# A state-space scan after a convolution on one core: projections moved between the scan's steps

## The chip, the core and the metric

The kernel runs on one core of a Trainium2 chip. Five engines work side by side, each through its own queue and in its own order: TensorE (PE, matrix products into PSUM), VectorE (DVE), ScalarE (ACT, activation functions by loaded tables), GpSimd (POOL[...]) and SyncE (SP, which issues DMAs here). They wait for each other on semaphores. The metric is the device time of one execution in microseconds (us); lower is better. All data is 32-bit floating point.

## The reference

The input x is 8 images of 128 channels by 128 x 128. Layer 0 (a dilated convolution, 2D Fourier transforms, an attention over channels and a gate) gives an x of the same shape; the change doesn't touch it. Layer 1 is:

```python
y = conv3x3(x, conv_w) + conv_b
seq = y.reshape(B * H * W, 8, 16)              # 8 tokens of 16 numbers, from consecutive values along W
xi, z = split(seq @ in_proj_w.T)               # 32 each
xc = silu(causal_conv_over_tokens(xi, conv1d_w) + conv1d_b)
dt, Bm, Cm = split(xc @ x_proj_w.T, [1, 17])   # 1, 16, 16
dt = softplus(dt @ dt_proj_w.T + dt_proj_b)    # 32
h = 0
for l in range(8):                             # 32 x 16 states
    h = exp(dt[l] * A) * h + dt[l] * Bm[l] * xc[l]
    ys[l] = sum(h * Cm[l], over the 16)
out = ((ys + D * xc) * silu(z)) @ out_proj_w.T
result = x + silu(groupnorm(out reshaped to the image, 4 groups))
```

As a reader of the reference will see, the tokens of a sequence are 16 consecutive values of one image row, and its 8 tokens fill the row of one channel: channel and image row number the sequences. With channels and rows exchanged by a transposition, one block is 4 rows by 128 channels = 512 sequences.

## The kernel before

Layer 0 runs first (about 3.4 ms). Layer 1 then goes through 8 images x 32 blocks = 256 blocks. The scan of a block is cut in 16 steps, `s` = 0 to 15 (`NS`): token t = s // 2, and half of the 32 inner channels (two of four groups, `GP`) by s % 2. In a step, tiles are 128 partitions (8 channels x 16 states) by 1024 (two groups x 512 sequences). A half `hf` is 4 tokens. `step(i, s)` issues, in this order on each engine, parts of up to four blocks at once, and the order written there is the order of the queues: the body runs under a manual schedule for PE, ACT, DVE, POOL and SP, and the tile framework only adds the waits. For block i and step s:

- `spreads` (L517) for the step after this one: four small matmuls of 16 rows each that spread dt and u over the states, two into `da` (times A, L527) and two into `ups` (L528); then ACT's Exp on da (L530). For token 0 (steps 0 and 1) there is no previous state, so no da and no Exp: step 15 and step 0 issue no exponents. `ups` has one PSUM buffer of two banks, `da` two.
- `advance` (L540): for tokens after the first, DVE multiplies da by the state of two steps earlier (L551) and adds the new input (L552). In the steps of `ON_POOL` (5, 9, 13) the product goes to `ah` (L548) and POOL does the addition (L549).
- `inject` (L533): DVE multiplies ups by B (L537), for the step after this one, into a new h; `weigh` (L554): POOL multiplies h by C into hc (L558).
- `collect` (L561), every second step, four steps later: PE sums hc over the states into `yps` (L568); the first of a half is preceded by the product with D, `m_d` (L566). After the last of a half, `gated` (L572) multiplies by silu(z) on DVE.
- Around these, work of the neighbouring blocks: `project` (L479) for block i + 1 (x, dt, bc and z, each in two halves, one half per step from 0 to 7 by the table `FRONT`), `project_out` (L577) of block i - 1 in step 8, the image convolution `conv` (L460, table `CONV`) and the transposition `turn` (L471) of block i + 2 in steps 9 to 15. All of them take the one buffer of `misc` (L448, `pm`, one bank).
- `lay_out` (L501): SP copies dt, u, B and C of one half to the layout of the scan, in 16 DMAs of 64 or 256 KB. The first half of block i + 1 is laid out in step 8 of block i, the second in step 0 of its own block.
- `keep`, `norm_of` and the `last_...` functions (L588 to L637): statistics, a round trip of the output through DRAM and the final normalization, one block of the image before in each block.

dt, u and bc have one buffer for each half, xc, zs, ym, du, bb and cc have two, h six, hc seven.[...]

Of the kernel before, what the change touches and what calls it, by code (L numbers as in the profile page):

```python
# [9 lines left out]
F32 = mybir.dt.float32  # L10
AF = mybir.ActivationFunctionType
# [5 lines left out]
P = 128  # L17
C = 128
H = 128
W = 128  # L20
# [6 lines left out]
DI = 32  # L27
DS = 16
KC = 4
NG = 4  # L30
LP = 4
NH = 2
# [311 lines left out]
def layer1(ctx, tc, x1, w1, c1, out):  # L344
# [8 lines left out]
    nc = tc.nc  # L353
# [13 lines left out]
    def wf(name):  # L367
        at, n = W1[name]
        return wt[:, at:at + n]
# [13 lines left out]
    m_d = const.tile([P, P], F32, name="m_d")  # L383
# [5 lines left out]
    with tc.tile_pool(name="l1_prep", bufs=2) as prep:  # L389
# [19 lines left out]
        for hf in range(NH):  # L409
            for l in range(L):  # L410
                k = hf * L + l
# [4 lines left out]
    m_xh = m_x.rearrange("p f d l -> p f (d l)")  # L416
    m_zh = m_z.rearrange("p f g l d -> p f (g l d)")
    m_dtf = m_dt.rearrange("p d l -> p (d l)")
# [7 lines left out]
    RB = 4  # L426
    N = RB * C
# [1 line left out]
    NS = L * NG // GP  # L429
    wk1 = ctx.enter_context(tc.tile_pool(name="l1_w1", bufs=1))  # L430
    wk2 = ctx.enter_context(tc.tile_pool(name="l1_w2", bufs=2))
    hp = ctx.enter_context(tc.tile_pool(name="l1_h", bufs=6))
    hcp = ctx.enter_context(tc.tile_pool(name="l1_hc", bufs=7))
    p_u = ctx.enter_context(tc.tile_pool(name="l1_pu", bufs=1, space=PSUM))
    p_a = ctx.enter_context(tc.tile_pool(name="l1_pa", bufs=2, space=PSUM))
    p_m = ctx.enter_context(tc.tile_pool(name="l1_pm", bufs=1, space=PSUM))
# [3 lines left out]
    nb = len(blocks)  # L440
    st8 = [{} for _ in blocks]
    xins, stats, gns, tails = {}, {}, {}, []
    ON_POOL = (5, 9, 13)

    def live(i):
        return 0 <= i < nb

    def misc():  # L448
        return p_m.tile([P, RB, W], F32, name="pm")

    def load(i):
        b, r = blocks[i]
        if r % CH == 0:
            lo, hi = max(0, r - 1), min(H, r + CH + 1)
            xin = wk2.tile([P, CH + 2, W], F32, name="xin")
            nc.sync.dma_start(xin[:, :hi - lo, :], x1[b][:, lo:hi, :])
            xins[b, r // CH] = xin, lo
        st8[i]["xin"] = xins[b, r // CH]
# [17 lines left out]
        d["yT"] = wk1.tile([P, N], F32, name="yT")  # L476
        nc.scalar.copy(d["yT"], ps.rearrange("p a b -> p (a b)"))

    def project(i, what, hf):  # L479
        d = st8[i]  # L480
        ps = misc().rearrange("p a b -> p (a b)")
        if what == "x":
            nc.tensor.matmul(ps, m_xh[:, hf, :], d["yT"], start=True, stop=True)
            d["xc", hf] = wk2.tile([P, N], F32, name=f"xc{hf}")
            nc.scalar.activation(d["xc", hf], ps, AF.Silu, bias=wf("conv1d_b"))  # L485
        elif what == "z":
            nc.tensor.matmul(ps, m_zh[:, hf, :], d["yT"], start=True, stop=True)  # L487
            d["zs", hf] = wk2.tile([P, N], F32, name=f"zs{hf}")
            nc.scalar.activation(d["zs", hf], ps, AF.Silu)
        elif what == "dt":  # L490
            nc.tensor.matmul(ps, m_dtf, d["xc", hf], start=True, stop=True)  # L491
            d["dt", hf] = wk1.tile([P, N], F32, name=f"dt{hf}")
            nc.scalar.activation(d["dt", hf], ps, AF.Softplus, bias=wf("dt_b"))  # L493
            d["u", hf] = wk1.tile([P, N], F32, name=f"u{hf}")
            nc.gpsimd.tensor_mul(d["u", hf], d["dt", hf], d["xc", hf])  # L495
        else:
            nc.tensor.matmul(ps, m_bcf, d["xc", hf], start=True, stop=True)  # L497
            d["bc", hf] = wk1.tile([P, N], F32, name=f"bc{hf}")
            nc.scalar.copy(d["bc", hf], ps)

    def lay_out(i, hf):  # L501

        d = st8[i]
        du = wk2.tile([P, LP, N], F32, name="du")
        bb = wk2.tile([P, LP, N], F32, name="bb")
        cc = wk2.tile([P, LP, N], F32, name="cc")
        for q in range(NG):
            for k, v, g in ((0, d["dt", hf], q), (8, d["u", hf], (q + GP) % NG)):
                nc.sync.dma_start(du[q * DI + k:q * DI + k + 8], v[g * DI:(g + 1) * DI, :])
        for lp in range(LP):  # L510
            for k, v in ((0, bb), (1, cc)):
                at = (k * LP + lp) * DS
                nc.sync.dma_start(  # L513
                    v[:, lp, :], d["bc", hf][at:at + DS, :].unsqueeze(1).broadcast_to([DS, 8, N]))
        d["du", hf], d["bb", hf], d["cc", hf] = du, bb, cc
# [17 lines left out]
    def inject(i, s):  # L533
        d, t = st8[i], s // 2
        bb, lp = d["bb", t // LP], t % LP
        h = hp.tile([P, GP, N], F32, name="h")
        nc.vector.tensor_mul(h, d["ups", s], bb[:, lp:lp + 1, :].broadcast_to([P, GP, N]))  # L537
        d["h", s] = h
# [15 lines left out]
    def weigh(i, s):  # L554
        d, t = st8[i], s // 2
        cc, lp = d["cc", t // LP], t % LP
        hc = hcp.tile([P, GP, N], F32, name="hc")
        nc.gpsimd.tensor_mul(hc, d["h", s], cc[:, lp:lp + 1, :].broadcast_to([P, GP, N]))  # L558
        d["hc", s] = hc

    def collect(i, t):  # L561

        d, hf, lp = st8[i], t // LP, t % LP
        if lp == 0:
            d["yps"] = p_y.tile([P, N], F32, name="yps")
            nc.tensor.matmul(d["yps"], m_d, d["xc", hf], start=True, stop=False, skip_group_check=True)  # L566
        for g in range(NG):
            nc.tensor.matmul(  # L568
                d["yps"][g * DI:(g + 1) * DI], gather[:, lp, :], d["hc", 2 * t + g // GP][:, g % GP],
                start=False, stop=(lp == LP - 1), skip_group_check=True)  # L570

    def gated(i, hf):  # L572
        d = st8[i]
        d["ym", hf] = wk2.tile([P, N], F32, name=f"ym{hf}")
        nc.vector.tensor_mul(d["ym", hf], d["yps"], d["zs", hf])

    def project_out(i):  # L577
        d = st8[i]
        ps = misc()
        for j in range(RB):  # L580
            for hf in range(NH):
                nc.tensor.matmul(  # L582
                    ps[:, j, :], d["ym", hf][:, j * C:(j + 1) * C], m_of[:, hf, :],
                    start=(hf == 0), stop=(hf == NH - 1))
        d["xr"] = wk2.tile([P, RB, W], F32, name="xr")
        nc.scalar.copy(d["xr"], ps)

    def keep(i):  # L588
        d, (b, r) = st8[i], blocks[i]
# [32 lines left out]
    def last_load():  # L622
        b, r, sc, bi = tails.pop(0)
        v = wk2.tile([P, RB, W], F32, name="v")
        res = wk2.tile([P, RB, W], F32, name="res")
        nc.sync.dma_start(v, gns[b][:, r:r + RB, :])
        nc.sync.dma_start(res, x1[b][:, r:r + RB, :])
        fin["now"] = b, r, sc, bi, v, res

    def last_act():  # L630
        b, r, sc, bi, v, res = fin["now"]
        nc.scalar.activation(v, v, AF.Silu, bias=bi, scale=sc)

    def last_sum():
        b, r, sc, bi, v, res = fin.pop("now")
        nc.gpsimd.tensor_add(res, res, v)
        nc.sync.dma_start(out[b, :, r:r + RB, :], res)  # L637

    FRONT = {0: ("x", 0), 1: ("x", 1), 2: ("dt", 0), 3: ("bc", 0), 4: ("dt", 1), 5: ("bc", 1),
             6: ("z", 0), 7: ("z", 1)}  # L640
    CONV = {9: (0, 2), 10: (2, 3), 11: (3, 5), 12: (5, 6), 13: (6, 8), 14: (8, 9)}

    def step(i, s):

        ni, ns = (i, s + 1) if s + 1 < NS else (i + 1, 0)
        if s == 0 and live(i):
            lay_out(i, 1)
        if s == 0 and live(i + 2):
            load(i + 2)
        if live(ni):  # L650
            spreads(ni, ns)
        if s in FRONT and live(i + 1):
            project(i + 1, *FRONT[s])
        if s == 8 and live(i - 1):
            project_out(i - 1)
        if s in CONV and live(i + 2):
            conv(i + 2, *CONV[s])
        if s == 15 and live(i + 2):
            turn(i + 2)
        if live(i):  # L660
            advance(i, s)
        if live(ni):
            inject(ni, ns)
        if live(i):
            weigh(i, s)

        gi, gs = (i, s - 4) if s >= 4 else (i - 1, s - 4 + NS)
        if gs % 2 == 0 and live(gi):
            collect(gi, gs // 2)
        if gs in (7, 15) and live(gi):  # L670
            gated(gi, gs // 8)
        if s == 8 and live(i + 1):
            lay_out(i + 1, 0)
        if s == 1 and tails:
            last_load()
        if s == 7 and fin:
            last_act()
        if s == 8 and fin:
            last_sum()
        if s == 9 and live(i - 1):  # L680
            keep(i - 1)
        if s == 15 and live(i - 1) and blocks[i - 1][1] + RB == H:
            norm_of(blocks[i - 1][0])

    E = mybir.EngineType
    with tc.manual_schedule(engines={E.PE, E.Activation, E.DVE, E.Pool, E.SP}):
        for i in range(-2, nb + 1):
            for s in range(NS):
                step(i, s)
    while tails or fin:  # L690
        if not fin:
            last_load()
        last_act()
        last_sum()


def network(tc, x, w0, w1, c0, c1, out):
# [79 lines left out]
```

## Time and profile before

| | |
|---|---|
| Median of 3 runs | 19010.8 us (18965.37 to 19032.3) |
| Profiled execution, its own time | 18927.41 us |
| Its span, first to last instruction | 18925.6 us |
| PE busy | 17631.7 us (93%) |
| DVE busy | 13871.6 us (73%) |
| POOL busy | 12629.5 us (67%) |
| ACT busy | 10176.7 us (54%) |
| PE's mean granted clock | 0.891 |
| DMA, mean share of 16 engines | 47.3% on the queue of SP |

Busy shares are means over both layers. A busy PE isn't a PE at its peak, since the ends of matmuls are modelled and PE's clock can be throttled. Each float32 matmul stands in the trace as two records. In a line of groups, the two numbers behind the bar are busy time and the mean duration of one in ns, then the idle time of that engine just before and what ended it. In a timeline the columns are start, duration, engine, line and operation, with the idle time before it in brackets.

### The profile page before, as it was taken

To read this page: it belongs to the slowest core of one execution; us is meant where nothing else is said; L and a number is where in the kernel's file an instruction comes from. 1 tells how busy PE (TensorE), PEld (TensorE's weight loads), DVE (VectorE), ACT (ScalarE), POOL (GpSimd) and SP (SyncE) were. 2 spreads that over 40 slices of the span, in tenths; PEclk is the share of its full clock that TensorE was granted. 3 is DMA by queue.
4 is the path that set the end of the run, shared out by engine and by line. 5 is a ranking of instruction groups with operands and counts; after the bars stand their busy time and mean duration, and the time that the engine had idled before them with its cause. 6 is when DMAs were issued, how large, how long until landed. Compare 5 with 4: busy or idle time off the path is not lost.

```text
span 18925.6 us, 214060 instructions
## 1 busy us (share of the span) xinstructions
PE 17631.7 (93%) x74920; PEld 6394.7 (34%) x74920; DVE 13871.6 (73%) x14203; ACT 10176.7 (54%) x10759; POOL 12629.5 (67%) x5892
## 2 busy tenths in 40 slices
PE   8999999999999999999999999999999999999996
PEld 3554553333333333333333333333333333333332
DVE  1441437888887888878888888878888878888885
ACT  1221225565565565565665565666565565565564
POOL 0010115777777777777877777777777777777776
PEclk9999999888888888888888888888888888888887
DMA  2222224554555555555555555555555555555554
GB/s 87 71 76 77 78 75 92 95 98 93 101 109 106 108 109 108 106 106 111 108 109 108 105 107 111 107 107 110 106 111 106 107 107 108 107 108 110 107 109 121
DMA packets 1075829, 1933.33 MB, mean 102 GB/s; under 512 B 123968, under 2 KB 255040, under 8 KB 1058368
## 3 DMA queue, kind: packets, MB, share of 16 engines
q1 hardware_dynamic: 1001472, 1850.17, 47.3%
q10 hardware_dynamic: 73280, 69.47, 1.3%
q8 instruction: 594, 9.73, 0.2%
q14 instruction: 483, 3.96, 0.1%
HBM read 375.64 MB, written 201.33 MB: 30 GB/s over the span
## 4 chain that ended last, share of the span: by engine, by line
PE 54%; DVE 7%; SPq 6%; POOL 5%; DMA 4%; ACT 4%; issue 3%; POOLq 0%; ACTq 0%; DVEq 0%
PE da L527 14%; PE yps L568 8%; PE pm L134 8%; PE ups L528 8%; SPq L513 6%; POOL hc L558 5%; PE pm L582 4%; PE pm L491 3%; PE yps L566 3%; PE pm L497 3%; DVE h L537 3%; DMA cc<-bc 2%; DVE da L551 2%; PE pm L487 2%; DMA bb<-bc 2%
## 5 line engine op out<-in xcount | busy, mean ns | idle before, releaser
L558 POOL TENSOR_TENSOR hc<-h,cc 128x1024 f32<-128x1024 f32 x4096 | 9578.2, 2356 | 1046.9 <-issue 671.2
L537 DVE TENSOR_TENSOR h<-ups,bb 128x1024 f32<-128x1024 f32 x4096 | 4987.1, 1218 | 2538.7 <-PE ups L528 1765.2
L530 ACT ACTIVATE da<-da 128x1024 f32<-128x1024 f32 x3584 | 3612.7, 1008 | 4562.6 <-PE ups L528 4546.2
L528 PE MATMUL ups<-du,m_u 16*128 16x512 f32 x16384 | 5185.2, 699 | 442.8 <-DVE h L537 438.5
L527 PE MATMUL da<-du,m_a 16*128 16x512 f32 x14336 | 5529.0, 683 | 11.4 <-DVE h L552 2.8
L551 DVE TENSOR_TENSOR da<-da,h 128x1024 f32<-128x1024 f32 x2816 | 3447.3, 1224 | 153.5 <-ACT da L530 129.3
L552 DVE TENSOR_TENSOR h<-da,h 128x1024 f32<-128x1024 f32 x2816 | 3448.1, 1224 | 96.7
L527 PEld LDWEIGHTS da<-du,m_a 16*128 16x128 f32 x14336 | 1700.8, 195 | 3351.2 <-issue 1476.8
L568 PE MATMUL yps<-hc,l_ct 128*32 128x512 f32 x16384 | 2633.3, 720 | 3.0 <-POOL hc L558 3.0
L134 PE MATMUL pm<-xin,l_wt 128*128 128x508 f32 (+1 forms) x4608 | 2368.0, 623 | 5.1 <-DMA l_wt<-w 4.4
L495 POOL TENSOR_TENSOR u<-dt,xc 128x512 f32<-128x512 f32 x512 | 651.1, 1272 | 2534.5 <-ACT dt L493 2445.4
L530 ACT ACT_TABLE_LOAD x1531 | 1964.3, 1283 | 27.6
L528 PEld LDWEIGHTS ups<-du,m_u 16*128 16x128 f32 x16384 | 1411.4, 197 | 1240.4 <-DVE h L537 1172.7
L549 POOL TENSOR_TENSOR h<-ah,h 128x1024 f32<-128x1024 f32 x768 | 1815.0, 2363 | 1.7
L134 PEld LDWEIGHTS pm<-xin,l_wt 128*128 128x128 f32 x4608 | 750.7, 189 | 1528.7 <-issue 1475.5
L272 POOL TENSOR_TENSOR xr<-xr,sq 128x512 f32<-128x512 f32 x128 | 160.7, 1267 | 1649.2 <-ACT sq L271 1604.7
L548 DVE TENSOR_TENSOR ah<-da,h 128x1024 f32<-128x1024 f32 x768 | 935.1, 1218 | 186.0 <-ACT da L530 181.9
L134 PE MATMUL cps<-xin,l_wt 128*64 128x500 f32 (+2 forms) x4608 | 1023.6, 583 | 38.7 <-issue 30.4
L491 PE MATMUL pm<-xc,m_dt 128*128 128x512 f32 x1024 | 838.4, 912 | 139.6 <-ACT xc L485 138.7
L222 DVE COPY fT<-tps 128x512 f32<-128x512 f32 x128 | 88.6, 692 | 1179.2 <-PE tps L221 1179.2
L568 PEld LDWEIGHTS yps<-hc,l_ct 128*32 128x32 f32 x16384 | 346.5, 116 | 1679.6 <-issue 1263.6
L497 PE MATMUL pm<-xc,m_bc 128*128 128x512 f32 x1024 | 601.9, 671 | 257.2 <-ACT dt L493 257.2
(146 smaller groups left out, 15341.6 us busy)
## 6 DMA issues: line engine op xcount, KB each, us to landing
bb<-bc SPq DMA_DIRECT2D x2048, 256.0 KB
cc<-bc SPq DMA_DIRECT2D x2048, 256.0 KB
du<-dt SPq DMA_DIRECT2D x2048, 64.0 KB
du<-u SPq DMA_DIRECT2D x2048, 64.0 KB
xin<-x SPq DMA_DIRECT2D x112, 640.0 KB
xin<-x SPq DMA_DIRECT2D x48, 1408.0 KB
gn<-xr SPq DMA_DIRECT2D x256, 256.0 KB
v<-gn SPq DMA_DIRECT2D x256, 256.0 KB
```

Source lines behind the costliest of these rows:

```text
L134: nc.tensor.matmul(out[:, a:b, wa:wb], wt[:, t, :], src[:, r + dy + a - base:r + dy + b - base, wa + dx:wb + dx], start=(n == 0), stop=(n ...
L491: nc.tensor.matmul(ps, m_dtf, d["xc", hf], start=True, stop=True)
L497: nc.tensor.matmul(ps, m_bcf, d["xc", hf], start=True, stop=True)
L527: nc.tensor.matmul(da[:, q], m_a[a:a + 16, :], du[a:a + 16, lp, :], start=True, stop=True)
L528: nc.tensor.matmul(ups[:, q], m_u[u:u + 16, :], du[u:u + 16, lp, :], start=True, stop=True)
L530: nc.scalar.activation(da, da, AF.Exp)
L537: nc.vector.tensor_mul(h, d["ups", s], bb[:, lp:lp + 1, :].broadcast_to([P, GP, N]))
L549: nc.gpsimd.tensor_add(h, ah, h)
L551: nc.vector.tensor_mul(da, da, before)
L552: nc.vector.tensor_add(h, da, h)
L558: nc.gpsimd.tensor_mul(hc, d["h", s], cc[:, lp:lp + 1, :].broadcast_to([P, GP, N]))
L568: nc.tensor.matmul(d["yps"][g * DI:(g + 1) * DI], gather[:, lp, :], d["hc", 2 * t + g // GP][:, g % GP], start=False, stop=(lp == LP - 1), ...
```

## The change

The projections are done for both halves at once, 1024 wide, in PSUM buffers of `da`. x and z of block i + 2 are projected in step 15 (before it: one half a step, of block i + 1, in steps 0, 1, 6 and 7), dt of block i + 1 in step 0 (before: steps 2 and 4), bc in steps 1 and 2 (before: 3 and 5). The product u = dt * xc goes from POOL, by halves, to DVE, in one. `project_out` is cut in two, steps 5 and 6. The product with D is moved from the first matmul of a half in yps to the last, just ahead of `gated`. `ON_POOL` has four steps instead of three. The convolution's and the transposition's steps, and those of the last normalization, are moved. Buffers: h five, hc six; xc and zs three of double width, dt and u two of double width, ym one for each half; bc0 and bc1 stay at one.

```diff
-    hp = ctx.enter_context(tc.tile_pool(name="l1_h", bufs=6))
-    hcp = ctx.enter_context(tc.tile_pool(name="l1_hc", bufs=7))
+    wk3 = ctx.enter_context(tc.tile_pool(name="l1_w3", bufs=3))
+    hp = ctx.enter_context(tc.tile_pool(name="l1_h", bufs=5))
+    hcp = ctx.enter_context(tc.tile_pool(name="l1_hc", bufs=6))
...
-    ON_POOL = (5, 9, 13)
+    ON_POOL = (5, 8, 11, 14)
...
-    def project(i, what, hf):
+    def halves(m, rhs):
+
+        ps = p_a.tile([P, NH, N], F32, name="da")
+        for hf in range(NH):
+            nc.tensor.matmul(ps[:, hf], m[hf], rhs[hf], start=True, stop=True)
+        return ps
+
+    def project_x(i):
+        d = st8[i]
+        ps = halves([m_xh[:, hf, :] for hf in range(NH)], [d["yT"]] * NH)
+        d["xc"] = wk3.tile([P, NH, N], F32, name="xc")
+        nc.scalar.activation(d["xc"], ps, AF.Silu, bias=wf("conv1d_b"))
+
+    def project_z(i):
+        d = st8[i]
+        ps = halves([m_zh[:, hf, :] for hf in range(NH)], [d["yT"]] * NH)
+        d["zs"] = wk3.tile([P, NH, N], F32, name="zs")
+        nc.scalar.activation(d["zs"], ps, AF.Silu)
+
+    def project_dt(i):
+        d = st8[i]
+        ps = halves([m_dtf] * NH, [d["xc"][:, hf, :] for hf in range(NH)])
+        d["dt"] = wk2.tile([P, NH, N], F32, name="dt")
+        nc.scalar.activation(d["dt"], ps, AF.Softplus, bias=wf("dt_b"))
+
+    def inputs(i):
+        d = st8[i]
+        d["u"] = wk2.tile([P, NH, N], F32, name="u")
+        nc.vector.tensor_mul(d["u"], d["dt"], d["xc"])
+
+    def project_bc(i, hf):
...
+        nc.tensor.matmul(ps, m_bcf, d["xc"][:, hf, :], start=True, stop=True)
+        d["bc", hf] = wk1.tile([P, N], F32, name=f"bc{hf}")
+        nc.scalar.copy(d["bc", hf], ps)
...
-            nc.tensor.matmul(d["yps"], m_d, d["xc", hf], start=True, stop=False, skip_group_check=True)
...
-                start=False, stop=(lp == LP - 1), skip_group_check=True)
+                start=(lp == 0), stop=False, skip_group_check=True)
+
+    def skip(i, hf):
+        d = st8[i]
+        nc.tensor.matmul(d["yps"], m_d, d["xc"][:, hf, :], start=False, stop=True, skip_group_check=True)
...
-    FRONT = {0: ("x", 0), 1: ("x", 1), 2: ("dt", 0), 3: ("bc", 0), 4: ("dt", 1), 5: ("bc", 1),
-             6: ("z", 0), 7: ("z", 1)}
-    CONV = {9: (0, 2), 10: (2, 3), 11: (3, 5), 12: (5, 6), 13: (6, 8), 14: (8, 9)}
+    CONV = {7: (0, 2), 8: (2, 3), 9: (3, 5), 10: (5, 6), 11: (6, 7), 12: (7, 8), 13: (8, 9)}
+    OUT = {5: (0, 5), 6: (5, 8)}
...
-        if s in FRONT and live(i + 1):
-            project(i + 1, *FRONT[s])
-        if s == 8 and live(i - 1):
-            project_out(i - 1)
+        if s == 15 and live(i + 2):
+            project_x(i + 2)
+        if s == 0 and "loaded" in fin:
+            last_act()
+        if s == 0 and live(i + 1):
+            project_dt(i + 1)
+        if s in (1, 2) and live(i + 1):
+            project_bc(i + 1, s - 1)
+        if s in OUT and live(i - 1):
+            project_out(i - 1, *OUT[s])
         if s in CONV and live(i + 2):
             conv(i + 2, *CONV[s])
-        if s == 15 and live(i + 2):
+        if s == 14 and live(i + 2):
             turn(i + 2)
         if live(i):
             advance(i, s)
         if live(ni):
             inject(ni, ns)
+        if s == 1 and live(i + 1):
+            inputs(i + 1)
         if live(i):
             weigh(i, s)
+        if s == 15 and live(i + 2):
+            project_z(i + 2)
...
+            if gs in (7, 15):
+                skip(gi, gs // 8)
+                gated(gi, gs // 8)
```

Left out of the diff: the loop runs three blocks ahead instead of two; the last normalization's load goes from step 1 to step 8, its Silu from step 7 to step 0 (between z's Silu and dt's Softplus in ACT's queue), its sum from step 8 to step 3; `keep` goes from step 9 to 7.

## The prediction

> **What bounds the kernel now.** I read the page's clock row and costliest groups, the trace around one block (10011.8 to 10074.7 us), the throttle's records, and the issue times of SP. Layer 1 does 256 blocks; three in turn repeat every 184.3 us, so one takes 61.4 us.
>
> ```profile
> PEclk9999999888888888888888888888888888888887
> L537 DVE TENSOR_TENSOR h<-ups,bb 128x1024 f32<-128x1024 f32 x4096 | 4987.1, 1218 | 2538.7 <-PE ups L528 1765.2
> L530 ACT ACT_TABLE_LOAD x1531 | 1964.3, 1283 | 27.6
> ```
>
> Eight tenths in layer 1: TensorE's clock is part of the bound. Steps 2 to 8 run at ScalarE's pace, two loads around each projection, and PE waits for the result:
>
> ```profile
> 10028.29 1.28 ACT L493 ACT_TABLE_LOAD   x1
> 10029.59 0.69 ACT L493 ACTIVATE dt<-pm,l_wt 128x512 f32<-128x512 f32 x1
> 10030.29 1.28 ACT L530 ACT_TABLE_LOAD   x1
> 10031.58 1.01 ACT L530 ACTIVATE da<-da 128x1024 f32<-128x1024 f32 x1
> ...
> 10030.33 1.12 PE L497 MATMUL pm<-xc,m_bc 128*128 128x512 f32 x2 [1.13 <-ACT dt L493]
> ```
>
> Steps 10 to 15 run at DVE's pace, starts 1.25 + 1.14 + 1.14 = 3.53 us apart, while PE is nearly full:
>
> ```profile
> 10057.45 1.22 DVE L551 TENSOR_TENSOR da<-da,h 128x1024 f32<-128x1024 f32 x1
> 10058.70 1.22 DVE L552 TENSOR_TENSOR h<-da,h 128x1024 f32<-128x1024 f32 x1
> 10059.84 1.21 DVE L537 TENSOR_TENSOR h<-ups,bb 128x1024 f32<-128x1024 f32 x1
> 10060.97 1.22 DVE L551 TENSOR_TENSOR da<-da,h 128x1024 f32<-128x1024 f32 x1
> ```
>
> Busy time by stretch (length; PE, PEld, DVE, ACT, POOL; clock; DMA share, GB/s), cut at the throttle's edges:
>
> ```profile
> 10015.41:10022.24 6.83, 6.83 (x18) 1.75 (x22) 1.22 (x1) 2.16 (x3) 5.88 (x3) 0.50 0.79 122
> 10022.24:10032.47 10.23, 8.50 (x43) 2.56 (x38) 8.85 (x8) 9.41 (x9) 2.12 (x2) 1.00 0.89 196
> 10032.47:10039.30 6.83, 6.83 (x23) 1.55 (x17) 4.77 (x5) 4.89 (x6) 5.32 (x4) 0.50 0.25 94
> ```
>
> The clock is whole or half. Matmuls at half clock lost this block 3.2, 2.4 and 1.7 us; 62.96 - 7.3 = 55.7 us at full clock (a two-window block: 58.4 - 3.4 = 55.0).
>
> I weighted matmul time by the array's rows and columns in use (16 of 128 rows in the spreads, 32 of 128 columns in the collects). Between 6000 and 15900 us, 412 full-clock windows before a drop had at most 0.46; of 1794 without a drop, 95% had over 0.56 and none under 0.44. Half clock ended after windows with at least 0.88 of their own time, 0.44 of the full rate. So each 3.41 us window needs some 1.5 us of full-array work; at half clock it must be nearly all dense work, which four spreads (2.1 us, worth 0.53) spoil.
>
> [...]
>
> **The change, part by part.** Let T = 0 be the end of inject(15); hand-offs 0.05 us.
>
> Loads: twelve per block (around x, dt, z twice each) become three in the instruction list: 9 x 1.28 = 11.5 us less ACT. Two 512-wide calls become one: about 0.3 us less, three times.
>
> DVE: u moves here (1.22, the 1024-wide row), a fourth POOL step removes one add (1.14). Even.
> POOL: minus 2.54, plus 2.36: even.
> PE: the same matmuls. x, z and dt (2.1 us each at full clock) go to steps 15 and 0; output, 2.05 us whole, to 5 and 6; convolution to 7 to 13. m_d moves behind the collects, and gated waits for it. In step 3 PE has room (m_d ends at 18.9, gated is due at 20.3). In step 11 it hasn't: spreads(12) starts when inject(11) ends, 1.05 us, then tap and m_d 2.1; DVE meanwhile needs only 2.49 to gated, so it waits 0.65 us. The other edges cost nothing: the output projection's halves lie in steps with room on PE, the copy to xr waits in ACT's idle time (ACT is busy some 25 us of the block once the loads are gone), and the fewer h and hc buffers suffice, since POOL is at most four steps behind DVE when inject(s+1) needs weigh(s-4), and the collect that frees a slot of hc stands two steps earlier in PE's queue. The prologue's extra round is a few us once.
>
> The boundary in a row, no longer under exponents:
> PE: collect until 0.35, spreads(0) to 1.4, x to 3.5, z to 5.6, spreads(1) to 6.7, dt to 8.8, collect to 9.8, spreads(2) to 10.9, bc0 to 11.9.
> ACT: x to 4.7, z to 6.7, last Silu (0.80) to 7.5, load to 8.8, Softplus 8.9 to 10.0, load to 11.3, exp(2) to 12.3.
> DVE: inject(2) 10.9 to 12.05, u to 13.25, then advance(2).
> From there DVE alone: nine steps of 3.53, four POOL steps of 2.49 (13 before), three of gated and bn_stats at 0.60: 31.8 + 10.0 + 1.8 = 43.6. Sum 56.85 us, with step 11's wait 57.5.
>
> A wait added: bc1 is copied in step 2 instead of 5, and still has one buffer, which lay_out(i,1) of step 0 is reading. Its DMAs now (T = 11.8):
>
> ```profile
> 10010.01 0.74 SPq L509 DMA_DIRECT2D du<-dt  x1
> ...
> 10026.01 1.58 SPq L513 DMA_DIRECT2D cc<-bc  x1
> ```
>
> By the DMA packets (2 KB, 256 of du and 1024 of bb and cc) the last lands at 10031, T + 19.2. After, spreads(15) frees du 0.5 us later, and cc waits for POOL's hc(15) at 6.0: T + 20.1. Behind the copy on ACT stands exp(4), for which DVE waits: 20.1 + 0.59 + 1.01 = 21.7 against 20.9 when advance(4) is due: 0.9. Bounds: 0 (landing under 19) to 5 (packets under load took 70 to 300 ns). Base: 58.4 us at full clock, about 3 over before's: the boundary's chain x, z, Softplus, exp, u holds DVE idle 7 us, where before's projections lay beside DVE's work.
>
> Clock A: steps 3 and 4 have only spreads with m_d or a collect, 2.1 us of 4.1 and 4.5: activity 0.33 to 0.46. The drop comes at 18 to 23 (three alignments of the window grid worked through). It is hidden until 25.3, inject(5); then PE sets the pace at half clock: spreads(6) 2.1, output 2.1, spreads(7) 2.1, output and collect 3.3, spreads(8) 2.1, convolution 4.0. The spreads stand at 25.3, 29.5 and 34.9, so a window dense enough comes only in the 3.3 or the 4.0. With window edges at 31.9 and 35.3 it is the former: spreads(8) then ends at 36.2 and inject(8) at 37.4, due at 34.85, 2.5 late. With edges at 36.4 and 39.8, or 37.5 and 41.0, it is the convolution: inject(9) ends at 42.6 or 43.2, due at 37.9, 4.7 or 5.3 late. Mean 4.2. DVE has no room to win it back. Bounds 0 and 8 (another two steps at half clock).
>
> Clock B: step 13 has spreads and one tap, 2.1 of 3.53: 0.39 to 0.46 by the alignment. I give it one half. The drop then comes about T - 1, and the next window free of spreads lies within x and z, which run on PE's path at half clock to about T + 8: 8.2 us at half cost 4.1, 2.05 on the mean.
>
> Sum: 58.4 + 4.2 + 2.05 = 64.65 us; 3.25 more per block, x 256 = 830 us on the profiled execution's 18,927 us (span 18,925.6). Layer 0 is untouched. That execution lies 83 us under the median of the runs; to that I add the same: 19,010.8 + 830 = about 19,840 us.
>
> **Rivals.** *The clock holds* (faster): steps 3 to 6 keep over 1.5 us of dense work in each window, because DVE's steps there are shorter than I made them. Place: ups L528 of steps 4 to 8; price: A and B go, 58.4 us, 256 x -3.0 = -770, 18,240; with A at 1.5 and no B, 59.9, 18,630. For it: over layer 1 (3524 to 18655 us) ACT was busy 9075 us, 37 of each block's 61.4, and 11.5 of these go. Against: the 10.23 us stretch above, PE idle 1.7 us, was followed by half clock. It decides from A + B under 3.0 us.
> *The DMA wait is long*: bb and cc land at T + 25, five us past advance(4)'s need, and PE idles until then. 4 us more per block: 20,880. For: DMA at 0.8 to 0.9 in just that stretch; against: the queue starts when it does now.
> *Gains and losses cancel*: A at 2.5 and B rare give 58.4 + 2.5 + 0.5 = 61.4, 19,010. For: before pays about 6 us to the clock too.
> That the loads stay is excluded by the instruction list.
>
> **How the numbers follow.** Forecast (62.7 to 66.3 us a block; 19,350 to 20,260): 0.55. Longer, mostly the DMA wait: 0.12. Cancelling (60.9 to 62.7; 18,900 to 19,350): 0.18, of which 0.06 within 0.3% (18,954 to 19,068, about what a measurement of this kernel can tell) and 0.02 below. Clock holds: 0.15. So faster 0.17, same 0.06, slower 0.77. The range leaves out some 0.10 under 18,800 and 0.10 above 20,350; the forecast's own is 19,350 to 20,260.
>
> **What would show it.** Table loads near 800; POOL without u; half clock in about a third of layer 1, with drops in steps 3 and 4; ACT's bc1 copy idle up to T + 20, released by DMA; ups L528 waiting for inject in steps 3 to 5. Wrong if the clock row shows nines in layer 1, if bc1's copy waits beyond T + 22, or if x and z don't follow each other on PE.

## The result, and the profile after

The changed kernel takes 19149.9 us (median; 19125.35 to 19192.02) against 18999.18 us for the kernel before on the same chip: ratio 1.0082, 95% interval 1.0056 to 1.0108. It is slower, as forecast, but by 0.8% where 4.4% were forecast, inside the wide range (18,800 to 20,350) and outside the likeliest case's own (19,350 to 20,260). The profiled execution of the changed kernel (span 19190.2 us) happens to be its longest; per block of the scan its mean is 62.73 us, that of the kernel before 61.76 us (means over all 255 distances between the ends of inject(15), image ends among them).

The page's clock row, one of its costliest groups, and the table loads among the groups by line, as before:

```profile
PEclk9999998888888888888888888888888888888886
L553 DVE TENSOR_TENSOR h<-ups,bb 128x1024 f32<-128x1024 f32 x4096 | 4993.9, 1219 | 2903.9 <-PE ups L544 2546.7
...
L546 ACT ACT_TABLE_LOAD x263 | 337.4, 1283 | 240.0 <-issue 206.9 <-PE ups L544 32.9
L491 ACT ACT_TABLE_LOAD x256 | 328.4, 1283 | 4.5
L503 ACT ACT_TABLE_LOAD x256 | 328.4, 1283 | 4.6
```

Three loads a block instead of twelve; ACT is busy 3144 us less. That bought no time: DVE's idle time before inject rose from 2539 to 2904 us (the part put down to PE from 1765 to 2547), and the clock row is no better (the granted clock of layer 1 fell from 0.878 to 0.844).

One block, from the end of inject(15) at T = 10020.45 us to the next at 10081.85 us. ACT and DVE at the boundary and behind it (start, duration, engine, line, operation, idle time before):

```profile
10029.89 1.11 ACT L503 ACTIVATE dt<-da,l_wt 128x1024 f32<-128x1024 f32 x1
10031.94 1.28 ACT L546 ACT_TABLE_LOAD   x1 [0.93 <-issue]
10033.24 1.01 ACT L546 ACTIVATE da<-da 128x1024 f32<-128x1024 f32 x1
...
10040.41 0.59 ACT L515 COPY bc<-pm 128x512 f32<-128x512 f32 x1 [4.74 <-DMA xin<-x]
10040.89 1.02 ACT L546 ACTIVATE da<-da 128x1024 f32<-128x1024 f32 x1
```

```profile
10028.02 1.23 DVE L553 TENSOR_TENSOR h<-ups,bb 128x1024 f32<-128x1024 f32 x1 [3.48 <-PE ups L544]
10032.01 1.23 DVE L553 TENSOR_TENSOR h<-ups,bb 128x1024 f32<-128x1024 f32 x1 [2.76 <-PE ups L544]
10033.15 1.22 DVE L508 TENSOR_TENSOR u<-dt,xc 128x1024 f32<-128x1024 f32 x1
...
10041.34 0.68 DVE L594 TENSOR_TENSOR ym<-yps,zs 128x512 f32<-128x512 f32 x1
10041.94 1.23 DVE L567 TENSOR_TENSOR da<-da,h 128x1024 f32<-128x1024 f32 x1
...
10047.84 1.22 DVE L553 TENSOR_TENSOR h<-ups,bb 128x1024 f32<-128x1024 f32 x1 [1.14 <-POOL hc L574]
10052.31 1.23 DVE L553 TENSOR_TENSOR h<-ups,bb 128x1024 f32<-128x1024 f32 x1 [0.85 <-PE ups L544]
10057.17 1.23 DVE L553 TENSOR_TENSOR h<-ups,bb 128x1024 f32<-128x1024 f32 x1 [1.24 <-PE ups L544]
```

And PE across the block's end, then its spreads for inject(6):

```profile
10018.43 0.73 PE L544 MATMUL ups<-du,m_u 16*128 16x512 f32 x1
10019.09 1.11 PE L476 MATMUL pm<-l_ct,y 128*128 128x128 f32 x4
10020.14 1.94 PE L583 MATMUL yps<-hc,l_ct 128*32 128x512 f32 x8
10022.00 1.18 PE L544 MATMUL ups<-du,m_u 16*128 16x512 f32 x4
10023.12 1.98 PE L484 MATMUL da<-yT,m_x 128*128 128x512 f32 x4
10024.94 1.88 PE L484 MATMUL da<-yT,m_z 128*128 128x512 f32 x4
...
10046.64 1.06 PE L544 MATMUL ups<-du,m_u 16*128 16x512 f32 x1
```

The order of the prediction's boundary is all there. inject(2) starts at T + 11.6 (forecast 10.9), bc1's copy at T + 20.0, when a DMA ends ACT's idle time (forecast 20.1), advance(4) at T + 21.5 (21.7). Then three injects in a row wait while PE is at half clock. The view puts the first of these waits down to POOL, but POOL's product ended at 10047.0, and the last spread that this inject reads at 10047.7. The busy time by stretch, cut where the granted clock changes (columns as before):

```profile
10018.75:10022.16 3.41, 3.41 (x17) 1.07 (x14) 3.10 (x4) 2.88 (x3) 3.33 (x3) 0.50 0.11 43
10022.16:10042.64 20.48, 19.88 (x78) 6.02 (x82) 13.71 (x13) 10.45 (x11) 13.32 (x6) 1.00 0.75 154
10042.64:10056.29 13.65, 13.61 (x52) 5.88 (x56) 11.20 (x10) 3.61 (x4) 10.94 (x7) 0.50 0.11 41
10056.29:10080.19 23.90, 23.61 (x108) 6.74 (x100) 22.10 (x20) 7.74 (x8) 20.49 (x9) 1.00 0.69 131
```

The prediction's two drops (stretches at half clock) are there, A at T + 22 for four windows of 3.413 us, B at T - 1.7 for one. The stretches add up to 61.44 us, exactly 18 windows of 3.413 us. The windows are read from the traces: from 4000 us on the granted clock of both kernels is 0.5 or 1.0, and every change of it (1232 before, 959 after) lies within 0.01 us of one grid of 3.413 us.

### The profile page after: what moved, and what is told of

Read it like the earlier page. It is cut to its first block, busy times and chain, and to the rows that moved or that the text cites. A ratio compares the mean times of both kernels' runs of the same rounds, so it can differ in the third digit from the quotient of the medians.

```text
span 19190.2 us, 208781 instructions
## 1 busy us (share of the span) xinstructions
PE 18443.3 (96%) x74920; PEld 6645.5 (35%) x74920; DVE 13878.4 (72%) x14203; ACT 7032.3 (37%) x7703; POOL 12632.6 (66%) x5636
## 5 line engine op out<-in xcount | busy, mean ns | idle before, releaser
L543 PE MATMUL da<-du,m_a 16*128 16x512 f32 x14336 | 6343.9, 728 | 210.0 <-DVE h L568 193.2
L544 PE MATMUL ups<-du,m_u 16*128 16x512 f32 x16384 | 5410.2, 737 | 9.7 <-DVE h L553 2.6
L568 DVE TENSOR_TENSOR h<-da,h 128x1024 f32<-128x1024 f32 x2560 | 3134.0, 1224 | 87.8
L567 DVE TENSOR_TENSOR da<-da,h 128x1024 f32<-128x1024 f32 x2560 | 3132.2, 1224 | 65.0 <-ACT da L546 62.8
L583 PE MATMUL yps<-hc,l_ct 128*32 128x512 f32 x16384 | 2824.9, 769 | 1.7 <-POOL hc L574 1.7
L565 POOL TENSOR_TENSOR h<-ah,h 128x1024 f32<-128x1024 f32 x1024 | 2420.7, 2364 | 392.0 <-DVE ah L564 391.8
L564 DVE TENSOR_TENSOR ah<-da,h 128x1024 f32<-128x1024 f32 x1024 | 1240.9, 1212 | 0.0
L602 PEld LDWEIGHTS pm<-m_o,ym 128*128 128x128 f32 x4096 | 909.7, 327 | 767.1 <-issue 766.3
L602 PE MATMUL pm<-m_o,ym 128*128 128x128 f32 x4096 | 1060.1, 440 | 0.6 <-DVE ym L594 0.6
L515 ACT COPY bc<-pm 128x512 f32<-128x512 f32 x512 | 301.6, 589 | 1041.0 <-DMA cc<-bc 594.9
```

What stands on the lines that cost most here:

```text
L543: nc.tensor.matmul(da[:, q], m_a[a:a + 16, :], du[a:a + 16, lp, :], start=True, stop=True)
L544: nc.tensor.matmul(ups[:, q], m_u[u:u + 16, :], du[u:u + 16, lp, :], start=True, stop=True)
L564: nc.vector.tensor_mul(ah, da, before)
L565: nc.gpsimd.tensor_add(h, ah, h)
L567: nc.vector.tensor_mul(da, da, before)
L568: nc.vector.tensor_add(h, da, h)
```

## The experiments

Theory: at full clock the changed block is about 58.4 us against 55 to 56 before (its boundary is a chain on which DVE waits, with a DMA wait and D's wait behind it), and half clock adds to both. Rivals: half clock is only a by-product of waits; or the clock alone makes the difference; or the table loads did set the pace before, and the gain was eaten elsewhere. The means per block and the half-clock time per block are from each run's trace, the ratios to the kernel before from the runs timed beside each.

| run | median us | ratio (95%) | us per block | of it half clock |
|---|---|---|---|---|
| before | 18999.2 | | 61.76 | 15.0 |
| changed | 19149.9 | 1.0082 (1.0056-1.0108) | 62.73 | 19.6 |
| before_fill | 17462.1 | 0.9187 (0.9169-0.9204) | 56.03 | 1.1 |
| before_thin | 18418.6 | 0.9722 (0.9701-0.9743) | 59.73 | 9.3 |
| before_exp | 18229.9 | 0.9590 (0.9576-0.9605) | 59.03 | 12.1 |
| before_fill_exp | 17349.3 | 0.9162 (0.9148-0.9175) | 55.60 | 1.6 |
| fill_a | 18914.2 | 0.9951 (0.9935-0.9966) | 61.63 | 10.8 |
| fill_ab | 18959.7 | 0.9983 (0.9974-0.9991) | 61.78 | 11.2 |
| fill_all | 18109.8 | 0.9567 (0.9552-0.9581) | 58.50 | 0.7 |
| fill_all_bc | 17873.5 | 0.9439 (0.9424-0.9453) | 57.60 | 0.5 |
| fill_all_d | 18618.6 | 0.9828 (0.9791-0.9865) | 60.53 | 5.4 |
| fill_bc_d | 18033.1 | 0.9518 (0.9499-0.9537) | 58.24 | 0.5 |
| fill_bc_d2 | 17817.5 | 0.9400 (0.9383-0.9416) | 57.40 | 0.5 |
| bc_two | 18914.0 | 0.9983 (0.9976-0.9991) | 61.72 | 17.7 |

**Holding the clock with work that nothing uses.** In the changed kernel's `spreads`, a dense matmul into the bank of da that the spread is about to overwrite:

```diff
+        if s in (4, 5, 6):
+            for q in range(1):
+                nc.tensor.matmul(da[:, q], m_bcf, d["xc"][:, 0, :], start=True, stop=True)
         for q in range(GP):
             g = k * GP + q
```

> The changed kernel with one more dense matmul (128 rows, 512 columns, 1.05 us at full clock) on PE ahead of the spreads of tokens' steps 4, 5 and 6, written into the da bank that the spread overwrites; its result is used by nothing. PE has 1.5 to 3 us of idle time there. Clock theory (half clock in steps 4 to 8 costs the block 3 to 4 us, because PE does too little in steps 3 and 4): the drop that began 22 us after inject(15) goes, block 62.7 to about 59.5 us, time about 18,400 (18,200 to 18,600). Rival, the chain of waits alone sets the time and half clock is its by-product: within 0.3% of the changed kernel, 19,100 to 19,200. Rival, PE is full: 3 x 1.05 us more per block, 19,950.

Measured 18914 us, not 18,400. Drop A is gone from 246 of 255 blocks, but B now lasts three windows in those 246, and the block is 61.44 us again: 18 windows. With `(4, 5, 6, 14, 15)`:

> As before it, and such matmuls ahead of the spreads of steps 14 and 15 too, where the second drop (in steps 13 and 14) comes from. Clock theory: no drop is left or nearly none, block near the full-clock sum of 57.5 to 58.4 us, time about 18,000 (17,850 to 18,250), clock in layer 1 above 0.95. Rival, only the first drop costs: as fill_a, 18,400. By-product rival: 19,100 to 19,200.

Measured 18960 us. B is gone and A is back, at T + 25. The 13 blocks without any drop took 57.71 us. So neither first forecast held: taking away one drop let the other grow. I put A's return down to idle time of PE between step 4's collect and the next da bank, an estimate; fill_all puts two more matmuls there, at the end of step 4:

```diff
+        if s == 4 and live(i):
+            ps = misc().rearrange("p a b -> p (a b)")
+            for k in range(2):
+                nc.tensor.matmul(ps, m_bcf, st8[i]["xc"][:, k, :], start=True, stop=True)
```

> The changed kernel with dense matmuls that nothing uses ahead of the spreads of steps 4, 5, 6, 14 and 15 (one each, into da) and two more at the end of step 4 (into pm), so that no 3.4 us window on PE is nearly empty. Theory that the arrangement itself is longer at full clock (57.5 us a block by the prediction's sum without its DMA wait, against 55.5 measured for the kernel before with its own fill): 17,462 + 2.0 x 256 = 17,975 (17,900 to 18,100), no half clock but at image ends. Rival, only the clock makes the change slower: 17,460 or less. With the 0.9 us DMA wait: 18,200.

Measured 18110 us, with no drop in 244 of 255 blocks, which took 58.2 us on the mean. That is the changed kernel's block at full clock, DMA wait and all; the forecast's base was 58.4. Nothing of it is the price of the two matmuls in step 4, which lie behind the DMA wait: inject(6) follows inject(5) at DVE's own pace, 2.5 us. The same with the kernel before, one matmul ahead of five of its spreads:

```diff
+        if s in (1, 3, 4, 5, 9):
+            w = da if t else p_a.tile([P, GP, N], F32, name="da")
+            nc.tensor.matmul(w[:, 0], m_bcf, d["xc", 0], start=True, stop=True)
```

> The kernel before with the same extra dense matmul ahead of the spreads of steps 1, 3, 4, 5 and 9 (5 x 1.05 us of PE a block), where its own low windows lie. Clock theory: drops mostly gone, from 61.7 to 56 to 59 us, 17,550 to 18,300. Rival, PE full in these steps or ACT's loads the bound whatever the clock: the matmuls come on top or change nothing, 19,000 to 20,300.

Measured 17462 us, below the expected range: 8.1% faster than the kernel before by adding work to its busiest engine. From its page, and the stretch of one block:

```profile
PEclk9999999999999999999999999999999999999997
L540 DVE TENSOR_TENSOR h<-ups,bb 128x1024 f32<-128x1024 f32 x4096 | 4983.7, 1217 | 1070.8 <-PE ups L531 957.0
L530 PE MATMUL da<-du,m_a 16*128 16x512 f32 x14336 | 4726.0, 644 | 1.8 <-DVE h L555 1.7
```

```profile
10000.00:10055.50 55.50, 53.74 (x256) 17.96 (x259) 50.20 (x45) 36.85 (x39) 48.00 (x23) 1.00 0.62 125
```

55.50 us a block in 229 of 255 blocks, all at full clock, and DVE's idle time before inject down from 2539 to 1071 us. DVE is now busy 50.2 of 55.5. The kernel before itself has five blocks without a drop in its trace, and they take 55.48 us: so the unused matmuls change the clock and hardly anything else. Half clock is thus no by-product: it costs the kernel before 5.7 us a block (61.76 - 56.03) and the changed one 4.2 (62.73 - 58.50). And the clock isn't all: at full clock the changed block is 2.5 us longer.

Is it the array's activity, or just a busy PE? The same five matmuls with 16 rows instead of 128:

```diff
-            nc.tensor.matmul(w[:, 0], m_bcf, d["xc", 0], start=True, stop=True)
+            o = k * GP * 32
+            nc.tensor.matmul(w[:, 0], m_a[o:o + 16, :], d["xc", 0][o:o + 16, :], start=True, stop=True)
```

> The kernel before with the five extra matmuls of before_fill in the same places and of the same length (512 columns), but of 16 rows instead of 128. Theory that the clock goes by how much of the array works (rows and columns weighted): an eighth of the activity each, the drops stay, 18,700 to 19,600. Rival, the time that PE is busy counts, or the extra instructions change the order of waits: near before_fill's 17,462.

Measured 18419 us, below the expected range: about a third of before_fill's gain for as many instructions of the same length (ratios 0.9722 and 0.9187). 65 blocks had no drop and took 55.48 us; most others kept two drops. So rows count. That an eighth of the rows gives a third of the gain is no contradiction, for the traces show a limit. They were weighted as in the prediction, each matmul record with 0.53 us for 512 columns at full clock (half of the 1061 ns that the median dense record took at half clock), times its shares of the array's rows and columns, as a share of the window. The limit of 0.46, which the prediction had from the kernel before alone, tells whether the next window is at half or full clock in all but 213 of the 55,150 windows of the 13 other kernels (from 4000 us to the last block). Over all 14 kernels the best single limit, 0.465, fails in 248 of 59,481 windows; on rows alone it fails in 2303, on PE's busy share in 6280. By that weighting a thin matmul adds an estimated 0.04 to a window (two records of 0.53 us, / 8 / 3.41), and of the kernel before's 614 windows ahead of a drop 168 lay within 0.04 of the limit; 346 drops are left in before_thin, 27 in before_fill.

**What the table loads cost.** Silu as Identity, Softplus as Exp in layer 1 (z and the last normalization likewise), so these kernels compute other values; they leave out the loads:

```diff
-            nc.scalar.activation(d["xc", hf], ps, AF.Silu, bias=wf("conv1d_b"))
+            nc.scalar.activation(d["xc", hf], ps, AF.Identity, bias=wf("conv1d_b"))
...
-            nc.scalar.activation(d["dt", hf], ps, AF.Softplus, bias=wf("dt_b"))
+            nc.scalar.activation(d["dt", hf], ps, AF.Exp, bias=wf("dt_b"))
```

> The kernel before with layer 1's Silu replaced by Identity and Softplus by Exp, so that ACT loads no table inside a block (computation changed: the activations of x, z, dt and of the last normalization are other functions; same instructions otherwise). Theory that the loads set the pace of steps 2 to 8: twelve loads, 15.4 us of ACT, go; PE no longer waits for the projections, block 61.7 to 56 to 58.5 us, time 17,550 to 18,200. Rival, the loads lay beside work that is needed anyway: block over 60.5, time over 18,700.

> The kernel before with the fill matmuls, and Silu as Identity and Softplus as Exp in layer 1 (other functions, no table load inside a block). What twelve loads cost when the clock holds. If they lie beside DVE's and PE's work, as the 0.5 us waits of DVE for ACT suggest: 1 to 2 of them show, block 54.5 to 55.3, 17,200 to 17,420. If they set the pace of steps 2 to 8: block under 53.5, under 16,950.

Without the loads the kernel before takes 18230 us (between the two forecasts). With the clock held, 17349: the typical block goes from 55.50 to 54.82 us. Twelve loads, 15.4 us of ACT a block, show as 0.7 us: they lie beside DVE's work. Of the 2.7 us that they cost with the clock free (61.76 - 59.03), the larger part, 2.7 - 0.7 = 2.0 us, goes with the clock (half clock fell from 15.0 us a block to 12.1); why it fell isn't shown. So there was little in the loads for the change to win.

**The DMA wait.** Two buffers for each half of bc, in the changed kernel and in fill_all:

```diff
-        d["bc", hf] = wk1.tile([P, N], F32, name=f"bc{hf}")
+        d["bc", hf] = wk2.tile([P, N], F32, name=f"bc{hf}")
```

> As fill_all, with two buffers for each half of bc, so that bc1's copy in step 2 no longer waits for the DMAs that read the block before's. The prediction's term: 0.9 us a block, 230 us less than fill_all. Rival, read from the changed kernel's trace (advance(4) started when gated ended, not later): the wait is hidden, within 50 us of fill_all.

> The changed kernel with two buffers for each half of bc and nothing else. With the clock held this was worth 0.9 us a block (18,110 to 17,874). Reading of the changed kernel's trace: under half clock at the block's start the copy comes late anyway and advance(4) is not held up, so nothing is gained: 19,050 to 19,200. Rival, the prediction's sum, where waits and clock add up: 18,920.

With the clock held: 58.50 - 57.60 = 0.90 us, the forecast's number, though not its sum, as the table below shows. In fill_all's view of the waits ACT's copy stands with these lines (us in total, times, longest); in fill_all_bc its waits for DMA come to 16 us in all:

```profile
ACT bc L515 <- DMA cc<-bc: 1099.0, 175, 7.7
...
ACT bc L515 <- DMA xin<-x: 145.9, 21, 16.3
```

Alone in the changed kernel, two buffers save 1.0 us a block (62.73 to 61.72), where I had expected nothing. Medians over blocks of one kind show where the two savings come from (us after T; the last column is the block's length):

| blocks | inject(2) | bc1's copy | inject(5) | next T |
|---|---|---|---|---|
| fill_all, no drop (244) | 10.1 | 20.1 | 24.1 | 58.2 |
| fill_all_bc, no drop (246) | 10.1 | 14.1 | 22.5 | 57.3 |
| changed, B of one window (167) | 11.5 | 20.1 | 24.1 | 61.6 |
| changed, B of three windows (82) | 14.4 | 19.9 | 26.8 | 64.3 |
| bc_two, B of one window (238) | 11.6 | 15.5 | 23.9 | 61.4 |

With the clock held, the DMA wait holds inject(5) back by 1.6 us, not 0.9; in fill_all_bc the unused matmuls of step 4, now uncovered, take 0.7 us back before inject(6) (DVE waits 0.92 us there, 0.20 in fill_all). Under half clock the wait and B lie in one chain, and the copy stands at T + 20.1 with B or without it: a B of one window makes inject(2) 1.4 us late, and the DMA wait swallows all of it. In bc_two, where nothing swallows it, inject(5) comes 1.4 us later than in fill_all_bc, and a block of that kind is only 0.2 us shorter than the changed kernel's. Most of its 1.0 us is that the long drops went: 85 of 255 blocks of the changed kernel have a B of three windows or more, 13 of bc_two. Why they went isn't shown; the typical block of bc_two, 61.46 us on the mean in 217 blocks, is 18 windows long.

**D last.** In fill_all, then in fill_all_bc, the product with D first in yps as before the change; fill_bc_d and fill_bc_d2 have one more unused matmul in step 3, where it had stood, and the latter one less in step 4:

```diff
         if lp == 0:
             d["yps"] = p_y.tile([P, N], F32, name="yps")
+            nc.tensor.matmul(d["yps"], m_d, d["xc"][:, t // LP, :], start=True, stop=False, skip_group_check=True)
...
-                skip(gi, gs // 8)
                 gated(gi, gs // 8)
```

> As fill_all, with the product with D first in yps again, as before the change. Theory that D last costs DVE 0.65 us in step 11, where gated waits for it: 165 us less than fill_all. Rival, the matmul is missed or paid in step 12 instead: within 50 us of fill_all.

> As fill_all_bc, with the product with D first in yps again, and one more unused dense matmul at the end of step 3, where the product with D had stood, so that the clock holds there. D last costs 0.65 us in step 11 by the prediction: block 57.3 to 56.7, 17,874 - 165 = 17,710. Rival, the wait moves to step 12, where PE now has one matmul more: within 50 us of 17,874.

> As fill_bc_d, with one unused matmul in step 4 instead of two, so that steps 3 and 4 hold as much PE work as in fill_all_bc (the product with D has taken the place of one there). fill_bc_d's trace has DVE's 0.64 us wait for yps in step 11 gone, 0.51 us more in step 14 and 1.05 us more before inject(6), where the extra matmul stood. Theory that the order of D moves the wait and hardly its sum: block 57.1 to 57.4, within 50 us of fill_all_bc's 17,874. Prediction's term alone: 17,710. If D first is dearer in itself: 18,000.

fill_all_d was inconclusive: taking the matmul out of step 3 brought drop A back at T + 19 in 198 blocks (18619 us), and the 56 blocks without a drop took 58.1 us, as in fill_all. fill_bc_d came out slower (18033), for the extra matmul in step 4 stood before inject(6), where DVE waited 1.97 us against 0.92. fill_bc_d2 holds the work of steps 3 and 4 equal: typical block 57.14 against 57.32, 0.2 us (56 us by the timed runs, just over the 50 of the forecast). DVE's waits say where the rest went. The first line is fill_all_bc, the second fill_bc_d2 (times are those of two executions):

```profile
10040.99 0.69 DVE L597 TENSOR_TENSOR ym<-yps,zs 128x512 f32<-128x512 f32 x1 [0.64 <-PE yps L592]
```

```profile
10028.55 1.22 DVE L556 TENSOR_TENSOR h<-ups,bb 128x1024 f32<-128x1024 f32 x1 [0.51 <-PE ups L547]
```

gated's 0.64 us is gone and 0.51 us stand before inject(15), put down to its spreads on PE. From step 12 to there PE's queue holds the product with D and two unused matmuls, of steps 13 and 14. So with this fill the wait moved. Whether D first would keep its 0.64 us where nothing unused stands in PE's way wasn't run without the drops.

## Why the prediction was right or wrong

- *Loads, engines' sums*: right. Three loads a block; DVE 13,878 us against 13,872; POOL even.
- *Boundary*: right in order, and 0.8 us shorter than forecast: at full clock inject(2) starts at T + 10.1, not 10.9. ACT's three 1024-wide calls (x, z, dt), which the row has at 1.1 to 1.2 us, took 1.11, 1.02 and 1.11 in the changed kernel's block.
- *DMA wait, 0.9*: right in cause, and bc1's copy stands at T + 20.1 as forecast. That exp(4) stands behind it on ACT is shown by the block above: the copy starts at 10040.41, exp(4) at 10040.89, and advance(4) follows on DVE at 10041.94. Its price at full clock is 1.6, because the boundary before it is shorter; that the experiment gave 0.90 is luck, since unused matmuls hid the rest.
- *Step 11's wait, 0.65*: right in the trace (0.64). As a price of D last it isn't settled: with the fill, D first pays 0.51 of it in step 14.
- *Base 58.4*: right as a sum, 58.2 in the blocks of fill_all without a drop; the boundary's - 0.8 and the DMA wait's + 0.7 cancel. For before's 55.0 to 55.7, 55.48 and 55.50. That PE would go to half clock in steps 3 and 4 held too, and when, in the blocks with B of one window (T + 21.9; forecast 18 to 23).
- *Clock A 4.2 and B 2.05*: the step that failed. Together they cost 62.73 - 58.50 = 4.2 us where 6.25 stood. A came in nearly every block and cost 3.4: from inject(5) to the next T a block takes 37.5 us, with B of either length, against 34.1 in fill_all. I had given three alignments of the window grid one weight each; the block settles on the grid (140 of 255 blocks have B of one window and A of four, 79 B of three and A of four, and nearly all others are variants of these), and both kinds are cheaper than the mean of the three. B's full price was right, 4.3 us at inject(2) where it lasts three windows (forecast 4.1), but it did so in a third of the blocks. B came in nearly every block and not in half of them, but in two thirds it was over by about T + 1.4. For I wrote that "the next window free of spreads lies within x and z", and the turn and the collect of step 14 are free of spreads as well: 1.11 and 1.94 us at half clock, one after the other. And I added B to a base that already holds the DMA wait. They lie in one chain, ahead of advance(4): of B's 1.4 us nothing is left at inject(5), of its 4.3 us 2.7. So B cost 2.7 in a third of the blocks, 0.9 on the mean.
- *Three blocks for the mean*: 61.4 where the layer's mean, with image ends, is 61.76.

The terms close: forecast + 3.25 us a block; - 2.05 for the clock (- 0.8 for A and - 1.2 for B), - 0.35 for before's mean, + 0.1 for the base: + 0.95, measured 62.73 - 61.76 = + 0.97. The change lost less to the clock than the kernel before (4.2 against 5.7), although it spends more time at half clock (19.6 us a block against 15.0). The rival "gains and losses cancel" was nearest in its number, not in its terms (A at 2.5, B rare); "the clock holds" had the right price and the wrong premise, as the runs with fill show.

## What to carry to other kernels

Where TensorE's clock row isn't full, hold the clock first, even with matmuls that nothing uses in PE's idle gaps (here they took 8.1% off the kernel before), and judge other edits after that: a change that takes work from an engine beside the path can come with another share of half clock (without the loads, 12.1 us a block instead of 15.0). To find where, add up each window's matmul time weighted by the rows and columns that it uses, which here told the next window's clock in all but 0.4% of the windows, at a limit of 0.46. Price a removed cost with the clock held (12 loads, 15.4 us of ACT, were worth 0.7), but look at what the unused matmuls hide or delay themselves (0.7 of the DMA wait's 1.6). Don't add up clock drops as if they were independent: taking one away can lengthen the next (in fill_a, B from one window to three), and a drop ahead of a fixed wait on the same chain is partly swallowed by it (here 1.4 us of 1.4, or 1.6 of 4.3). When a projection is moved forward, look at what its output buffer still feeds; one more buffer for bc was worth more here (0.9) than D's place (0.2).

## What the runs showed of the hardware

Five unused float32 matmuls a block made the kernel before 8.1% faster. The longest idle time of PE in any of the 1093 windows ahead of a drop, in the kernel before and the changed one, was 3.06 us (before, 5011.47 to 5014.88 us: PE busy 0.35 of 3.41), and 449 of the changed kernel's 479 such windows had under 0.35 us of it: a busy PE was no protection. What told the next window's clock was how much of the array worked in each window of 3.413 us: under about 0.46 of it by the weighting above, the next window was at half clock, over it at full clock, in all but 0.4% of the windows of 14 kernels. The 0.46 is in the durations of these traces, where the ends of matmuls are modelled. From 4000 us on half clock came in multiples of 3.413 us (in the kernel before and the changed one 616 and 480 stretches, all but the changed kernel's last, which runs past its span), and blocks settled on 18 such windows, 61.44 us, in kernels as different as fill_a (246 of 255 blocks) and bc_two (217).
